# Attention scores in parts of five and one chunk, maxima over three operands, later biases, and a last row sum on TensorE

## The chip, the core and the metric

The program runs on one NeuronCore of a Trainium2 chip. The metric is the device time of one execution in microseconds (us); the median of three executions of the kernel before is 2793.07 us (2792.54 to 2796.49). All arithmetic is 32-bit floating point. Engine names follow the profile: PE is TensorE's matmul side (PEld its weight loads), DVE VectorE, ACT ScalarE, POOL GpSimd, SP the engine that issues most of the loads.

## The reference, cut to what matters

Four blocks follow each other on `x` of 16 batches, 100 tokens and 512 channels. Each adds its output, times the tanh of a gate, to `x`: cross-attention with 16 heads (called a0 below), a mixture of eight experts with two per token, cross-attention with 8 heads (a1), and a feed-forward layer with dequantized weights. Each works on the layer-normalized `x`. The context of 722 rows and 384 channels is the same for both attentions. What the change touches is the attention:

```python
q = layernorm(x) @ Wq + bq          # a1 has no bq, bk, bv
k = ctx @ Wk + bk                   # 722 keys per batch
v = ctx @ Wv + bv
attn = softmax(q @ k.T * D**-0.5)   # over the 722 keys, per head
x = x + tanh(g) * ((attn @ v) @ Wo + bo)
```

## The kernel before, in words

**Tiling.** The 1600 tokens lie in 13 tiles of 128 rows (the last has 64). The 722 keys of a batch are six chunks (`NS`), five of 128 keys and one of `SL` = 82. A *step* is one pair of batch `b` and 128-channel block `m`; 16 batches by 4 blocks are 64 steps in each attention. A block holds `G` heads: four in a0, two in a1.

**One step.** `scores(b, m, part)` multiplies keys by queries, so that keys lie on the partitions and the 100 tokens on the free side. Part 0 has chunks 0 to 2, part 1 has chunks 3 to 5 (`NS2` = 3). Each part takes one PSUM tile `ps_s` with one bank per head (a0 has one such tile, a1 two). ACT copies it to the SBUF tile `raw` (L379, and L385 and L388 for part 1; L388 is the chunk of 82), and a DVE reduction (L391) takes the greatest over the chunks. The result of part 0 is put between the chunks, so that the reduction of part 1 goes over four operands and gives `mx`. `peaks` (L393) transposes `mx` on PE (`ps_mx`, L399) and reduces to one maximum for each token and head. `softmax` (L407) transposes the maxima back to all partitions (`ps_top`, L413), subtracts them in two DVE instructions of three chunks (L417), takes the exponential on ACT (L423), and adds the six chunks on POOL to `sm` (L426, five adds). `attend` (L431) multiplies by the values (L438), sums `sm` over the partitions with a matmul by ones (L447), and divides on DVE (L455, L456). The rows of the last chunk past 82 hold a very negative number, so their exponential is zero.

**The order.** PE's order is the order in which the program is written. On the other engines the framework's scheduler orders the instructions when the program is built; an instruction handed to `keep_in_program_order` keeps its written place. Every engine executes its queue in order. `run` (L490) writes the steps one behind the other: iteration `i` has `peaks(i)`, part 0 of the scores of step `i+1`, filler units, `softmax(i)` (in a0), part 1 of the scores, `attend(i-1)`, further filler units. In a1 both score parts and `attend` stand ahead of the first fillers and `softmax`. The fillers are keys and values of the next batches (L210, L232), queries (L334), the query inputs (L314) and `project` (L458), the output projection of a tile with its addition to `x`. Units with a due step are in `extra`; the others are dealt out by a planner so that each step gets an equal share of matmul columns:

```python
whole = sum(map(self.cost, todo + sum((extra[j] for j in range(i, end)), [])))
share = whole / max(1, end - i)
```

with `end` = 62. The first units with at least 2000 columns of a step go to the first place (`u[0]`), the others to the second (`u[1]`). All of these take PSUM tiles of the pool `ps_m`, which has four buffers. `project` of the tiles that batch `b` completes stands at step `4(b+1)+1`; in a0 the layer norm and the routing logits of that tile for the experts follow it (`after_project`).

**Biases.** `add_bias` (L330) adds the gated output bias to a tile of `x` on POOL. In a0 each `query_input` calls it right behind its normalization. In a1 the first four tiles get it as units of step 3. The gated bias is made by `output_bias` (L298) on PE and DVE.

Of the kernel before, what the change touches and what calls it, by code (L numbers as in the profile page):

```python
# [16 lines left out]
P = 128  # L17
B, T, C = 16, 100, 512
# [5 lines left out]
KC = C // P  # L24
KK = CK // P
NS = -(-S // P)
SL = S - (NS - 1) * P
NS2 = NS // 2
GB = 4
GT = GB * T  # L30
EPS = 1e-5
# [19 lines left out]
def bcast(ap, *shape):  # L51
    return ap.to_broadcast(list(shape))
# [7 lines left out]
def rows_of(i):  # L60
    return P if i < NTT - 1 else NL
# [81 lines left out]
class Attention:  # L143
# [167 lines left out]
            nc.vector.tensor_tensor(self.gbo, ps, self.gbo, ALU.add)  # L311
        nc.vector.tensor_scalar(self.gbo, self.gbo, self.gate, None, ALU.mult)

    def query_input(self, i, on_act=False):  # L314
        net, nc, n = self.net, self.net.nc, rows_of(i)
        xn = self.p2.tile([P, C], F32, tag="xn", name=f"xn_{self.name}_{i}")
        if on_act:
            nc.scalar.activation(
                xn,
                net.x[:, i, :],  # L320
                AF.Identity,
                bias=net.shift[:, i : i + 1],
                scale=net.rstd[:, i : i + 1],
            )
        else:
            net.normalized(nc.gpsimd, xn, i)
            self.add_bias(i)
        net.transposed(self.ps_m, self.tT[:, :, i * P : i * P + n], xn[:n])

    def add_bias(self, i):  # L330
        x = self.net.x[:, i, :]
        self.net.nc.gpsimd.tensor_tensor(x, x, self.gbo, ALU.add)

    def queries(self, g, m, lo=0, hi=GT):  # L334

# [22 lines left out]
    def scores(self, b, m, part):  # L358


        nc, D, G = self.net.nc, self.D, self.G
        g, i = divmod(b, GB)
        q = slice(i * T, (i + 1) * T)
        ps = self.ps_s.tile([P, G, 512], F32, tag="s", name="ps_s")
        for n in range(NS2):
            c = part * NS2 + n
            r = P if c < NS - 1 else SL
            for j in range(G):
                nc.tensor.matmul(  # L369
                    ps[:r, j, n * T : (n + 1) * T],  # L370
                    self.kT[b, m][j * D : (j + 1) * D, c * P : c * P + r],
                    self.qT[g][j * D : (j + 1) * D, m, q],
                    start=True,
                    stop=True,
                )

        st = self.raw[(b * KC + m) % 2]
        if part == 0:
            nc.scalar.copy(  # L379
                st[:, :, :NS2, :].rearrange("p g c t -> p g (c t)"), ps[:, :, : NS2 * T]  # L380
            )
            greatest, of = st[:, :, NS2, :], st[:, :, :NS2, :]
        else:
            n = NS2 - 1
            nc.scalar.copy(  # L385
                st[:, :, NS2 + 1 : NS, :].rearrange("p g c t -> p g (c t)"), ps[:, :, : n * T]
            )
            nc.scalar.copy(st[:SL, :, NS, :], ps[:SL, :, n * T : NS2 * T])  # L388
            self.mx[b, m] = self.p2.tile([P, G, T], F32, tag="mx", name="mx", bufs=1)
            greatest, of = self.mx[b, m], st[:, :, NS2:, :]  # L390
        nc.vector.tensor_reduce(greatest, of.rearrange("p g c t -> p g t c"), AX.X, ALU.max)  # L391

    def peaks(self, b, m):  # L393

# [12 lines left out]
    def softmax(self, b, m):  # L407

        nc, G = self.net.nc, self.G
        top, st = self.top.pop((b, m)), self.raw[(b * KC + m) % 2]  # L410
        ps = self.ps_m.tile([P, G, T], F32, tag="mm", name="ps_top")
        for j in range(G):
            nc.tensor.transpose(ps[:, j, :], bcast(top[:, j : j + 1], T, P), self.net.ident[:T, :T])  # L413
        t = self.p2.tile([P, 2, G, NS2, T], F32, tag="pT", name="pT")
        sm = self.p2.tile([P, G, T], F32, tag="sm", name="sm")
        for part in range(2):
            nc.vector.tensor_tensor(  # L417
                t[:, part],
                st[:, :, part * (NS2 + 1) : part * (NS2 + 1) + NS2, :],
                bcast(ps.unsqueeze(2), P, G, NS2, T),  # L420
                ALU.subtract,
            )
            nc.scalar.activation(t[:, part], t[:, part], AF.Exp)  # L423
            for n in range(NS2):
                if part or n:
                    nc.gpsimd.tensor_tensor(  # L426
                        sm, t[:, part, :, n, :], sm if part or n > 1 else t[:, 0, :, 0, :], ALU.add
                    )
        self.pT[b, m] = t, sm

    def attend(self, b, m):  # L431
        nc, D, G = self.net.nc, self.D, self.G
        t, sm = self.pT.pop((b, m))
        ps = self.ps_m.tile([P, 2, T], F32, tag="mm", name="ps_pv")
        for c in range(NS):
            n = P if c < NS - 1 else SL
            for j in range(G):
                nc.tensor.matmul(  # L438
                    ps[j * D : (j + 1) * D, 0, :],
                    self.v[b][:n, c, m * P + j * D : m * P + (j + 1) * D],  # L440
                    t[:n, c // NS2, j, c % NS2, :],
                    start=(c == 0),
                    stop=(c == NS - 1),
                )

        for j in range(G):
            nc.tensor.matmul(  # L447
                ps[j * D : (j + 1) * D, 1, :],
                self.net.ones[:, :D],
                sm[:, j, :],  # L450
                start=True,
                stop=True,
            )
# [36 lines left out]
    def run(self, done=(), after_project=None, more=()):  # L490
# [8 lines left out]
        for g in range(1, B // GB):  # L499
            at = 4 * KC * (g - 1)  # L500
# [27 lines left out]
        for i in range(-1, len(steps)):  # L528
            b, m = steps[max(i, 0)]
# [841 lines left out]
def tile_flamingo(ctx: ExitStack, tc: tile.TileContext, a: dict, out: bass.AP):  # L1371
    nc = tc.nc
# [15 lines left out]
    a0 = Attention(net, "a0", a["ctxT"], w0, tgx[:, 0:1], heads, extremes)  # L1388
    a1 = Attention(net, "a1", a["ctxT"], w1, tgx[:, 1:2], 8)
# [3 lines left out]
    with ExitStack() as cm:  # L1393
        pc = cm.enter_context(tc.tile_pool(name="moe_c", bufs=1))
        with ExitStack() as c0:
# [25 lines left out]
            with tc.manual_schedule(engines={PE}):  # L1421
                a0.first_keys()
                for f, *u in gates:
                    f(*u)
                for i in range(4):
                    net.moments(i)
                net.norm_scales(0, 4)
                for c in range(4):
                    a0.values(0, c)
                    if c == 2:  # L1430
                        a0.output_bias()
                for i in range(4):
# [12 lines left out]
                more = [(-1, a0.queries, 0, m) for m in range(1, KC)]  # L1445
                more += [(0, a0.values, 0, c) for c in range(4, NS)]
                a0.run((), after_project, more)

        with ExitStack() as c1:
# [3 lines left out]
            with ExitStack() as cw:  # L1453
                moe.open_weights(cw, 0)
                moe.open_rows(cw)
                with ExitStack() as cr:
                    ps = open_pool(cr, tc, "route_p", 6, space=PSUM)
# [10 lines left out]
                    with tc.manual_schedule(engines={PE}):  # L1468
                        late = range(LATE, NTT)
# [12 lines left out]
                        to = moe.places(ps, pn)  # L1482
# [9 lines left out]
                with tc.If(nc.values_load(flag[0:1, 0:1], min_val=0, max_val=1) > 0):  # L1492
                    guarded_attention(net, a["x"], a["ctxT"], w0, tgx[:, 0:1], heads, o_s, x_s)
                    with ExitStack() as cg:
                        p2 = cg.enter_context(tc.tile_pool(name="again_2", bufs=2))
                        pn = cg.enter_context(tc.tile_pool(name="again_n", bufs=1))
                        ps = cg.enter_context(tc.tile_pool(name="again_p", bufs=4, space=PSUM))
# [9 lines left out]
                        to = moe.places(ps, pn)  # L1507
# [99 lines left out]
```

## Time and profile before

| | |
|---|---|
| median of three runs | 2793.07 us |
| profiled execution | 2793.14 us |
| its span, first to last instruction | 2791.4 us |
| mean granted TensorE clock | 0.983 |
| PE busy | 2697.3 us (97%) |
| DVE, ACT, POOL busy | 1166.8, 855.9, 692.2 us |

Stages by the timeline, from the span's start: a0 to about 933 us, routing to about 980, the experts to about 1610, a1 to about 2418, the feed-forward layer to the end.

The page of a profile gives busy times and groups of instructions. A group's line has the count, the busy time, the mean duration of one in ns, and the idle time of the engine just before, with what ended it. A timeline row has start, length, engine, line, operation, and in brackets the idle time before it. The view of waits has in each row the waiting engine and line, what it waited for, the total in us, the number of waits and the longest. A window row has the stretch, its length, and for PE, PEld, DVE, ACT and POOL the busy time with the number of instructions, then the granted clock, the DMA share and GB/s.

### The profile page before, as it was taken

Reading aid. Unit: us, or ns where it says so; the run is one execution under the profiler, and the core shown is the slowest. Engines: PE = TensorE matmul, PEld = TensorE weight load, DVE = VectorE, ACT = ScalarE, POOL = GpSimd, SP = SyncE. Lnnn points to the kernel's source line nnn. Section 1 sums busy time; section 2 is a strip of 40 time slices with the busy share of each in tenths; the row PEclk is TensorE's granted clock in tenths of the full one; section 3 lists DMA queues with packets and bytes.
Section 4 is the critical chain, followed back from the end, with each engine's and each line's share of the span. In section 5 each row is a group of like instructions: output and inputs, shape, how many; then the busy total and the mean of one; then the engine's idle time right before and its main releaser. Section 6 shows DMA issues by size and latency. Waiting matters only on the chain. (4 is left out here: it accounts for less than half of the span.)

```text
span 2791.4 us, 45251 instructions
## 1 busy us (share of the span) xinstructions
PE 2697.3 (97%) x19536; PEld 1742.5 (62%) x19536; DVE 1166.8 (42%) x1449; ACT 855.9 (31%) x1322; POOL 692.2 (25%) x821
## 2 busy tenths in 40 slices
PE   8999999999998899999999989999999999799999
PEld 4565566566555588888878855666666666445554
DVE  4676767766667400000000056544444444521100
ACT  2445454444445100000000035433333334211110
POOL 3433434343333100000000054223222222401000
PEclk9999999999999899999999999999999999899999
DMA  4000100010001399999999522100001010430000
GB/s 155 25 17 18 33 25 25 17 44 18 17 29 43 121 342 344 318 314 319 317 319 310 189 77 59 36 17 18 32 17 33 17 33 1 146 95 15 12 12 10
DMA packets 129892, 278.31 MB, mean 100 GB/s; under 512 B 5825, under 2 KB 5841, under 8 KB 129169
## 3 DMA queue, kind: packets, MB, share of 16 engines
q1 hardware_dynamic: 117888, 246.80, 25.7%
q0 software_dynamic: 5088, 16.28, 1.8%
q10 hardware_dynamic: 6704, 12.19, 1.2%
q8 instruction: 159, 2.61, 0.4%
q14 instruction: 53, 0.43, 0.1%
HBM read 260.31 MB, written 14.94 MB: 99 GB/s over the span
## 5 line engine op out<-in xcount | busy, mean ns | idle before, releaser
L241 PE MATMUL ps_v<-wv_a,ctx_a 128*128 128x512 f32 (+1 forms) x1152 | 521.5, 600 | 0.4 <-PEq L923 0.4
L216 PE MATMUL ps_k<-ctx_a,wk_a 128*128 128x361 f32 x1488 | 487.2, 475 | 0.7 <-DVE tT_a L140 0.7
L426 POOL TENSOR_TENSOR sm<-pT,sm 128x400 f32<-128x400 f32 (+1 forms) x512 | 420.1, 820 | 44.2 <-ACT pT L423 4.8
L865 PE MATMUL ps_h<-xT,w 128*128 128x128 f32 x3712 | 422.1, 276 | 3.8 <-DVEq L1492 3.8
L865 PEld LDWEIGHTS ps_h<-xT,w 128*128 128x128 f32 x3712 | 419.5, 193 | 4.5 <-ACTq L1492 4.0
L216 PEld LDWEIGHTS ps_k<-ctx_a,wk_a 128*128 128x128 f32 x1488 | 274.7, 191 | 162.2 <-issue 20.1
L241 PEld LDWEIGHTS ps_v<-wv_a,ctx_a 128*128 128x128 f32 (+1 forms) x1152 | 205.6, 185 | 243.0 <-issue 234.0
L426 POOL TENSOR_TENSOR sm<-pT 128x400 f32<-128x400 f32 (+1 forms) x128 | 105.2, 822 | 928.4 <-ACT pT L423 928.3
L391 DVE TENSOR_REDUCE mx<-raw_a 128x400 f32<-128x1600 f32 (+1 forms) x128 | 287.2, 2244 | 80.2 <-ACT raw_a L388 74.0
L423 ACT ACTIVATE pT<-pT 128x1200 f32<-128x1200 f32 (+1 forms) x256 | 239.9, 953 | 260.5 <-DVE pT L417 260.1
L417 DVE TENSOR_TENSOR pT<-raw_a,ps_top 128x1200 f32<-128x1200 f32 (+1 forms) x256 | 268.0, 1085 | 33.0 <-PE ps_top L413 32.3
L369 PE MATMUL ps_s<-qT_a,kT_a 32*128 32x100 f32 (+3 forms) x4608 | 215.3, 279 | 2.9 <-ACT raw_a L379 1.6
L391 DVE TENSOR_REDUCE raw_a<-raw_a 128x400 f32<-128x1200 f32 (+1 forms) x128 | 152.0, 1187 | 138.6 <-ACT raw_a L379 138.3
L885 PE MATMUL ps_o<-w,midT 128*128 128x512 f32 x464 | 203.9, 592 | 0.0
L369 PEld LDWEIGHTS ps_s<-qT_a,kT_a 32*128 32x128 f32 (+3 forms) x4608 | 181.3, 181 | 35.9 <-issue 23.5
L876 DVE TENSOR_TENSOR midT<-silu,ps_h 128x512 f32<-128x512 f32 x58 | 39.9, 687 | 389.8 <-PE ps_h L865 389.8
L248 ACT COPY v_a<-ps_v 128x512 f32<-128x512 f32 x192 | 111.8, 584 | 292.7 <-PE ps_v L241 290.0
L1091 PE MATMUL ps_z<-ffn_w,y_ffn 128*128 128x512 f32 (+1 forms) x416 | 190.8, 594 | 0.0
L1073 PE MATMUL ps_y<-hT,ffn_w 128*128 128x384 f32 (+2 forms) x512 | 184.1, 504 | 0.0
L438 PE MATMUL ps_pv<-pT,v_a 128*32 128x100 f32 (+3 forms) x4608 | 163.7, 255 | 6.8 <-ACT pT L423 6.8
L837 POOL DMA_INDIRECT xt<-xn_d,map_i x29 | 27.5, 950 | 567.0 <-PE ps_xT L850 525.5
L379 ACT COPY raw_a<-ps_s 128x1200 f32<-128x1200 f32 (+1 forms) x128 | 116.3, 908 | 134.7 <-PE ps_s L369 133.2
(164 smaller groups left out, 2159.0 us busy)
## 6 DMA issues: line engine op xcount, KB each, us to landing
w<-in_L_ffn_w SPq DMA_DIRECT2D x116, 1024.0 KB, 6.5
w<-in_L_ffn_wo SPq DMA_DIRECT2D x29, 2048.0 KB, 10.5
ctx_a<-in_ctxT SPq DMA_DIRECT2D x30, 1083.0 KB, 5.4
q<-in_L_ffn_fc_q SPq DMA_DIRECT2D x8, 1024.0 KB, 5.0
ffn_w<-in_L_ffn_fc_scales SPq DMA_DIRECT2D x8, 1024.0 KB, 10.2
rows<-ot ACTq DMA_DIRECT2D x29, 256.0 KB, 6.8
xn_d<-xn_moe ACTq DMA_DIRECT2D x12, 256.0 KB, 2.0
ctx_a<-in_ctxT SPq DMA_DIRECT2D x6, 361.0 KB, 8.5
```

Source lines behind the costliest of these rows:

```text
L216: nc.tensor.matmul(ps, self.wk[:, k, m * P : (m + 1) * P], self.cxs[b][:, k, c * SH : (c + 1) * SH], start=(k == 0), stop=(k == KK - 1),)
L241: nc.tensor.matmul(ps[:n], self.cxs[b][:, k, c * P : c * P + n], self.wv[:, k, :], start=(k == 0), stop=(k == KK - 1),)
L369: nc.tensor.matmul(ps[:r, j, n * T : (n + 1) * T], self.kT[b, m][j * D : (j + 1) * D, c * P : c * P + r], self.qT[g][j * D : (j + 1) * D, ...
L391: nc.vector.tensor_reduce(greatest, of.rearrange("p g c t -> p g t c"), AX.X, ALU.max)
L417: nc.vector.tensor_tensor(t[:, part], st[:, :, part * (NS2 + 1) : part * (NS2 + 1) + NS2, :], bcast(ps.unsqueeze(2), P, G, NS2, T), ALU.su ...
L423: nc.scalar.activation(t[:, part], t[:, part], AF.Exp)
L426: nc.gpsimd.tensor_tensor(sm, t[:, part, :, n, :], sm if part or n > 1 else t[:, 0, :, 0, :], ALU.add)
L438: nc.tensor.matmul(ps[j * D : (j + 1) * D, 0, :], self.v[b][:n, c, m * P + j * D : m * P + (j + 1) * D], t[:n, c // NS2, j, c % NS2, :], s ...
L865: nc.tensor.matmul(ph[:, f, :], w[:, n, k, f * P : (f + 1) * P], self.xT[j][:, k, :], start=(k == 0), stop=(k == KC - 1),)
L885: nc.tensor.matmul(po, self.midT[j, f // 4][:, f % 4, :], w[:, f, :], start=(f == 0), stop=(f == KF - 1),)
L1073: nc.tensor.matmul(ps[:, :nt], w1[f // nf][:, k, f % nf * P : (f % nf + 1) * P], hT[g][:, k, :nt], start=(k == 0), stop=(k == KC - 1),)
L1091: nc.tensor.matmul(z[j][:n], y[:, j * P : j * P + n], w2[f // nf][:, f % nf, :], start=(f == 0), stop=(f == NF - 1),)
```

## The change

- **Scores.** Part 0 has five chunks (40 PE instructions in a0 for 24, since each product is two instructions in the trace), part 1 the last one. ACT copies part 0 with one instruction of 500 columns per head, part 1 with the copy of 82 rows.
- **Maxima.** Two reductions over three operands follow part 0 (chunks 0 to 2 into a slot; that slot with chunks 3 and 4 into `mx`). Part 1 adds one `tensor_tensor` maximum of `mx` and the last chunk.
- **Subtraction.** The second half is two instructions (two chunks, one chunk), since a slot lies between them now.
- **Last sums.** In the last two steps of an attention (`late`) POOL adds nothing; PE sums all six chunks by matmuls with ones.
- **Biases.** The first four tiles get theirs at steps 3 (tiles 0, 1) and 4 (tiles 2, 3), in both attentions, in written order on POOL.
- **Projection.** The tile that batch 14 completes (tile 10) is projected at step 63, no more at 61; in a0 its moments, scales, normalization, transposes and logits move by two with it.

```diff
-    def query_input(self, i, on_act=False):
+    def query_input(self, i, on_act=False, bias=True):
...
-            self.add_bias(i)
+            if bias:
+                self.add_bias(i)
...
-    def add_bias(self, i):
+    def add_bias(self, i, pin=False):
         x = self.net.x[:, i, :]
-        self.net.nc.gpsimd.tensor_tensor(x, x, self.gbo, ALU.add)
+        ins = self.net.nc.gpsimd.tensor_tensor(x, x, self.gbo, ALU.add)
+        if pin:
+            self.net.tc.keep_in_program_order(ins)
...
-        for n in range(NS2):
-            c = part * NS2 + n
-            r = P if c < NS - 1 else SL
+        r = SL if part else P
+        for n, c in enumerate((NS - 1,) if part else range(NS - 1)):
             for j in range(G):
                 nc.tensor.matmul(
...
-        if part == 0:
-            nc.scalar.copy(
-                st[:, :, :NS2, :].rearrange("p g c t -> p g (c t)"), ps[:, :, : NS2 * T]
-            )
-            greatest, of = st[:, :, NS2, :], st[:, :, :NS2, :]
-        else:
-            n = NS2 - 1
-            nc.scalar.copy(
-                st[:, :, NS2 + 1 : NS, :].rearrange("p g c t -> p g (c t)"), ps[:, :, : n * T]
-            )
-            nc.scalar.copy(st[:SL, :, NS, :], ps[:SL, :, n * T : NS2 * T])
-            self.mx[b, m] = self.p2.tile([P, G, T], F32, tag="mx", name="mx", bufs=1)
-            greatest, of = self.mx[b, m], st[:, :, NS2:, :]
-        nc.vector.tensor_reduce(greatest, of.rearrange("p g c t -> p g t c"), AX.X, ALU.max)
+        if part:
+            nc.scalar.copy(st[:SL, :, NS, :], ps[:SL, :, :T])
+            mx = self.mx[b, m]
+            nc.vector.tensor_tensor(mx, mx, st[:, :, NS, :], ALU.max)
+            return
+        nc.scalar.copy(st[:, :, :NS1, :].rearrange("p g c t -> p g (c t)"), ps[:, :, : NS1 * T])
+        mx = self.mx[b, m] = self.p2.tile([P, G, T], F32, tag="mx", name="mx", bufs=1)
+        for c, to in ((0, st[:, :, NS1, :]), (3, mx)):
+            nc.vector.tensor_reduce(
+                to, st[:, :, c : c + 3, :].rearrange("p g c t -> p g t c"), AX.X, ALU.max
+            )
...
+        late = b == B - 1 and m >= KC - 2
+        sm = None if late else self.p2.tile([P, G, T], F32, tag="sm", name="sm")
         for part in range(2):
-            nc.vector.tensor_tensor(
-                t[:, part],
...
+            for c, z, at in ((0, 3, 0),) if part == 0 else ((0, 2, 3), (2, 3, NS)):
+                nc.vector.tensor_tensor(
+                    t[:, part, :, c:z, :],
+                    st[:, :, at : at + z - c, :],
+                    bcast(ps.unsqueeze(2), P, G, z - c, T),
+                    ALU.subtract,
+                )
             nc.scalar.activation(t[:, part], t[:, part], AF.Exp)
-            for n in range(NS2):
+            for n in () if late else range(3):
...
+        parts = [sm] if sm is not None else [t[:, c // 3, :, c % 3, :] for c in range(NS)]
+        for k, of in enumerate(parts):
+            for j in range(G):
+                nc.tensor.matmul(
+                    ps[j * D : (j + 1) * D, 1, :],
+                    self.net.ones[:, :D],
+                    of[:, j, :],
+                    start=(k == 0),
+                    stop=(k == len(parts) - 1),
+                )
...
-                at = (b + 1) * KC + 1
+                at = (b + 1) * KC + (1 if b != B - 2 else KC - 1)
...
-                    a0.query_input(i)
+                    a0.query_input(i, bias=False)
...
+                more += [(3 + i // 2, a0.add_bias, i, True) for i in range(4)]
...
-            more += [(3, a1.add_bias, i) for i in range(4)]
+            more += [(3 + i // 2, a1.add_bias, i, True) for i in range(4)]
```

More of the change, by code (lines that the diff above doesn't have):

```diff
@@ L27 @@
 SL = S - (NS - 1) * P
-NS2 = NS // 2
+NS1 = NS - 1
 GB = 4
@@ L413, in softmax @@
             nc.tensor.transpose(ps[:, j, :], bcast(top[:, j : j + 1], T, P), self.net.ident[:T, :T])
-        t = self.p2.tile([P, 2, G, NS2, T], F32, tag="pT", name="pT")
-        sm = self.p2.tile([P, G, T], F32, tag="sm", name="sm")
+        t = self.p2.tile([P, 2, G, 3, T], F32, tag="pT", name="pT")
+        late = b == B - 1 and m >= KC - 2
+        sm = None if late else self.p2.tile([P, G, T], F32, tag="sm", name="sm")
         for part in range(2):
-            nc.vector.tensor_tensor(
-                t[:, part],
-                st[:, :, part * (NS2 + 1) : part * (NS2 + 1) + NS2, :],
-                bcast(ps.unsqueeze(2), P, G, NS2, T),
-                ALU.subtract,
-            )
+            for c, z, at in ((0, 3, 0),) if part == 0 else ((0, 2, 3), (2, 3, NS)):
[5 more added lines that the diff above has]
+                )
             nc.scalar.activation(t[:, part], t[:, part], AF.Exp)
-            for n in range(NS2):
+            for n in () if late else range(3):
                 if part or n:
@@ L440, in attend @@
                     self.v[b][:n, c, m * P + j * D : m * P + (j + 1) * D],
-                    t[:n, c // NS2, j, c % NS2, :],
+                    t[:n, c // 3, j, c % 3, :],
                     start=(c == 0),
@@ L444, in attend @@
                 )
[L446 to L453, printed above, removed]
+        parts = [sm] if sm is not None else [t[:, c // 3, :, c % 3, :] for c in range(NS)]
[8 more added lines that the diff above has]
+                )
         rs = self.p2.tile([P, T], F32, tag="rs", name="rs")
```

## The prediction

> **What bounds the kernel now.** First the page's busy times and clock:
>
> ```profile
> PE 2697.3 (97%) x19536; PEld 1742.5 (62%) x19536; DVE 1166.8 (42%) x1449; ACT 855.9 (31%) x1322; POOL 692.2 (25%) x821
> PEclk9999999999999899999999999999999999899999
> ```
>
> PE is the bound, so only its idle time and its half-clock time can be won: summed over the trace 89.9 us of gaps, and a clock of 0.983. Next, PE's waits:
>
> ```profile
> PE ps_mx L399 <- DVE mx L391: 33.7, 31, 6.3
> PE ps_pv L447 <- POOL sm L426: 22.3, 10, 8.7
> PE ps_pv L438 <- ACT pT L423: 6.8, 7, 1.8
> ```
>
> The change works on all three. By windows, 25.4 us of the waits ahead of `ps_mx` lie between 60 and 887 us, in a0's steps; nearly all of the rest at the ends of a0 and a1. The timeline of the worst step (step 4) shows the chain:
>
> ```profile
> 114.96 2.72 DVE L417 TENSOR_TENSOR pT<-raw_a,ps_top 128x1200 f32<-128x1200 f32 x2
> ...
> 116.46 1.20 ACT L423 ACTIVATE pT<-pT 128x1200 f32<-128x1200 f32 x1 [1.35 <-DVE pT L417]
> ...
> 117.57 0.81 ACT L385 COPY raw_a<-ps_s 128x800 f32<-128x800 f32 x1
> ...
> 118.27 1.20 ACT L423 ACTIVATE pT<-pT 128x1200 f32<-128x1200 f32 x1
> ...
> 119.38 0.48 ACT L388 COPY raw_a<-ps_s 82x400 f32<-82x400 f32 x1
> ...
> 119.89 2.90 DVE L391 TENSOR_REDUCE mx<-raw_a 128x400 f32<-128x1600 f32 x1 [1.22 <-ACT raw_a L388]
> ...
> 122.84 1.09 PE L399 MATMUL ps_mx<-ident,mx 128*100 128x128 f32 x4 [3.82 <-DVE mx L391]
> ```
>
> Part 1's last copy stands behind both exponentials, and a 2.9 us reduction follows: 12.2 us from one `peaks` (110.64) to the next operand. Durations come from the groups by shape:
>
> ```profile
> L391 DVE TENSOR_REDUCE mx<-raw_a 128x400 f32<-128x1600 f32 x64 | 189.2, 2957 | 74.0 <-ACT raw_a L388 74.0
> L417 DVE TENSOR_TENSOR pT<-raw_a,ps_top 128x1200 f32<-128x1200 f32 x128 | 173.7, 1398 | 17.7 <-PE ps_top L413 17.5
> L391 DVE TENSOR_REDUCE raw_a<-raw_a 128x400 f32<-128x1200 f32 x64 | 98.0, 1532 | 66.7 <-ACT raw_a L379 66.5
> L417 DVE TENSOR_TENSOR pT<-raw_a,ps_top 128x600 f32<-128x600 f32 x128 | 94.2, 772 | 15.3 <-PE ps_top L413 14.8 <-POOL x L332 0.3
> L379 ACT COPY raw_a<-ps_s 128x1200 f32<-128x1200 f32 x64 | 74.1, 1158 | 97.7 <-PE ps_s L369 96.3 <-PE ps_k L216 1.4
> L385 ACT COPY raw_a<-ps_s 128x800 f32<-128x800 f32 x64 | 51.7, 807 | 3.1 <-PE ps_s L369 3.1
> ```
>
> **The clock, a rule weighed.** Windows around two of the waits:
>
> ```profile
> 797.00:801.90 4.90, 2.10 (x20) 1.14 (x22) 3.15 (x2) 2.28 (x5) 4.06 (x4) 1.00 0.01 2
> 802.00:805.30 3.30, 3.30 (x27) 2.54 (x20) 1.69 (x3) 1.16 (x1) 0.77 (x1) 0.50 0.00 0
> 856.00:860.00 4.00, 2.03 (x31) 1.23 (x29) 3.76 (x9) 0.56 (x1) 1.30 (x2) 0.99 0.00 0
> 860.00:863.40 3.40, 3.40 (x4) 1.44 (x5) 2.71 (x7) 1.16 (x1) 0.00 (x0) 0.51 0.02 5
> ```
>
> After gaps of 2.80 and 1.97 us PE ran at half rate for 3.4 us, losing 1.7 us each. The Trainium skill ("TensorE: Matmul & The Clock Gate", section "Why this matters for your kernels") warns of gaps above about 3 us. By that rule only the 3.82 us gap (half rate from 122.7 to 129.5) costs, 3.3 us; by the rows 6.7. I follow the rows: shortened gaps of 2 us still count as dangerous.
>
> **Part 1: a0's steps.** New chain. `peaks` 0.53; part 0's 40 instructions at 24 in 0.93: 1.55; to the copy 0.12; the copy, by the slope from 800 to 1200 elements (0.88 ns each), 1.86; two reductions 3.06; subtractions 1.40, and by their slope (1.04 ns, 0.15 fixed) 0.98 and 0.56: 2.94, behind the reductions since these are written first; the maximum, 0.56 by the same slope. The last copy (0.47) is ready under the subtractions. With 0.05 for the semaphore: 10.7 us.
>
> Here a rule speaks against the change. The skill ("SBUF — State Buffer", section "SBUF: two separate sides") says that a DVE operation with two SBUF inputs and a POOL operation exclude each other for a whole instruction. The subtraction has one input in PSUM; the new maximum has both in SBUF and meets POOL's adds (1.04 us each). The trace has one such meeting:
>
> ```profile
> 1640.86 4.54 POOL L332 TENSOR_TENSOR x<-x,gbo_a 128x512 f32<-128x512 f32 x3 [3.77 <-DVE gbo_a L312]
> 1641.63 1.43 DVE L948 SCALAR_TENSOR_TENSOR x<-r,probs,x 128x512 f32<-128x512 f32 x1
> 1651.99 0.60 PE L447 MATMUL ps_pv<-sm,ones 128*64 128x100 f32 x4 [8.74 <-POOL sm L426]
> ```
>
> 0.74 alone became 1.43. By the page the loss is 0 to 1.04, by the row 0.69; I take 0.6: chain 11.3 us.
>
> PE's own step is `peaks` and part 0 (2.1), `ps_top`, part 1 and `attend` (0.44 + 0.3 + 1.35 = 2.1), and fillers at 0.842 ns per column (0.431 us per 512). It waits where 4.2 + fillers < 11.3, below 8430 columns. Working the planner's rule through for both versions: moving `project` out of `range(i, end)` lightens the tail. New columns: step 4 4844 (as before), 57 7522, 58 7010, 59 8310: waits 3.0 + 0.8 + 1.2 + 0.1 = 5.1. The 25.4 us become 5: **−20.3**. The page's worst case (chain 11.7) gives back 4, no meeting wins 2.
>
> Clock: 6.7 lost now; step 4 still gaps: **−4.5** (−3.3 to −6.7).
>
> What is late next: `ps_top` is held until the subtractions end, now 8.1 us after part 0 instead of about 6. In eleven steps with three or four short fillers the third may come for its buffer at 7.6. From 0 to 11 us; I take **+5**, since rotation is not visible in the rows.
>
> Part 1's matmuls in a0 need the only `ps_s` back: copy done at 0.12 + 1.86 + 0.05 = 2.03 after part 0; with one key filler PE comes at 2.29 (72.83 to 75.12). Hidden by 0.26; 0 to +5, taken as 0. In a1 two tiles exist, `peaks` waits nowhere in mid-stage, and the extra DVE instructions (0.35 for the maximum, 0.15 for the split) lie in a queue that is busy about half of the time: nothing.
>
> **Part 2: a0's start.** POOL's normalization of tile 2 began at 38.93 behind two biases (36.46, 2.49 us); PE waited 2.99 and 0.78. Without them the copies of tiles 0 and 1 on DVE end at 38.95, two more (0.69 each) at 40.3, queries start at 40.4 instead of 42.20: 1.8. PE ran at clock 0.53 from 41 to 48; one of its two half stretches should go, 1.7. **−3.5** (−1.8 to −4.8). At steps 3 and 4 the biases take 2.6 us each of a POOL queue that has 5.2 us of adds and 2.1 of query input in a step of 8 to 13; the sum made there is wanted one step later, so they are hidden; uncovered they would cost up to 5.
>
> **Part 3: a0's end,** 885.0 to 933.5 us, 48.5 us now: 26.8 of full-rate work, 12.8 waits, 8.9 half clock. New: sums on PE, 48 instructions for 8, about 0.85 each: 28.5. Waits: step 61 has 4332 columns, 3.4; step 63's part 1 behind the long copy with no filler, 1.6 (0.53 now); `peaks` of 63 3.8 (4.72 now); exponentials 1.7; `turn` of tile 10, whose moments, scales (ACT table load 1.28) and POOL pass now stand right ahead of it, 1.2. POOL's 3.56 goes; `project` fills step 63. Two table loads (896.4 and 903.3, 1.28 each) leave ACT's way between the exponentials. The store of the normalized tile on ACT's queue (2.0 us to landing) moves too; the gathers that read it start at 966.6, some 20 us behind. Half clock about 5. **−3** (−8 to +3).
>
> **Part 4: a1's start.** The five adds (0.68 each) can begin at 1642 instead of 1645.4; with two gathers (0.96) between them they end at 1647.3, not 1652: 4.7 less. Half rate then meets 5 us of work, +0.8; biases at step 4, a short step whose POOL idle is 1.55 against 2.6 us, +1. **−3** (−8 to +2).
>
> **Part 5: a1's end,** 2379.97 to 2409.64, 29.7 us.
>
> ```profile
> 2397.19 0.67 PE L399 MATMUL ps_mx<-ident,mx 128*100 128x128 f32 x2 [6.32 <-DVE mx L391]
> ```
>
> New: work 15.9 with PE sums; step 61's sum, still on POOL and with less filler ahead, 2.1; exponentials 3.6; feed-forward work on DVE between 1; half clock 3: 25.6, **−4** (−8 to +3). PE sums are in this work with 24 instructions for 4, 0.8 a step. SP's feed-forward loads start behind the last keys, as now (2387.5), and are first used at 2420: hidden.
>
> **Sum:** −20.3 − 4.5 + 5 − 3.5 − 3 − 3 − 4 = −33.3. Against the profiled execution, 2793.1 (span 2791.4 and 1.7 around it; the median is 2793.07): **2760 us**.
>
> **Rivals.** *DVE is the new wait:* the division (0.77 + 0.26) goes ahead of the maximum, chain 12.3. By the same table of steps the waits are 16, the buffers 11: 2777. For: DVE carries about 9 of 13 us in series. Against: the maximum is written first.
>
> *All stays covered:* −25.4 − 6.7 − 4.8 − 6 − 5 − 6, no buffer holds: 2739. Against: step 4's 4844 columns.
>
> *Slower: the last copy is queued on ACT behind the second exponential* in a0. Then it ends 9.9 us after part 0, the chain is 13.2, waits 44 us over 40 steps; with re-throttling and later buffers 2805. It decides from a chain of 13.1. For: ACT's queue is rebuilt. Against: above, the copy of 800 precedes that exponential, and the new copy is ready earlier.
>
> *It doesn't do what it says:* the rebuilt queues move the waits to other steps, 2793.
>
> **How the numbers follow.** 2760 case 0.56 (its own range 2749 to 2772), DVE 0.18, all covered 0.12, slower 0.10, no change 0.04. A measurement tells 0.2%, 5.6 us, from no change. Faster 0.86, same 0.04, slower 0.10. The range 2742 to 2786 leaves out the slower and unchanged cases and part of the covered one.
>
> **What would show it.** Right: `ps_mx` waits of about 5 us between 60 and 887; the 8.74 at a1's start halved; no wait on `sm` at either end. Wrong: over 12 us there, waits of `ps_k` or `ps_v` on `pT` or `rs`, `ps_s` waiting on `raw` in many steps, a copy of 82 rows behind the second exponential.

## The result, and the profile after

The changed kernel takes 2776.5 us (median; 2775.1 to 2779.0) against 2793.0: a ratio of 0.9939, 95% interval 0.9922 to 0.9957. It is faster by 16.5 us where 33.3 were forecast; the range of 2742 to 2786 holds it. The profiled execution's span fell from 2791.4 to 2774.3 us. First the page's busy times and clock, as shown of before:

```profile
PE 2695.3 (97%) x19656; PEld 1746.7 (63%) x19656; DVE 1091.4 (39%) x1705; ACT 859.8 (31%) x1194; POOL 685.1 (25%) x801
PEclk9999999999999999999999999999999999899999
```

DVE lost 75 us of work, but PE is the bound as before, and its mean clock rose only from 0.983 to 0.985. PE's waits (us in total, times, longest us):

```profile
PE ps_pv L452 <- POOL sm L429: 14.2, 8, 5.1
PE ps_mx L399 <- DVE mx L384: 11.9, 6, 3.7
PE ps_s L372 <- ACT raw_a L386: 11.5, 4, 4.4
PE ps_pv L441 <- ACT pT L426: 9.3, 7, 3.4
...
PE ps_k L216 <- DVE pT L420: 2.1, 2, 1.9
PE ps_y L467 <- DVE pT L420: 1.9, 1, 1.9
```

The 33.7 us on the maximum are 11.9 now, and the sums fell from 22.3 to 14.2. But the third row is nearly new: part 1 of the scores waits 11.5 us for the copy of part 0 to empty the only `ps_s`. The waits on exponentials grew from 6.8 to 9.3, and the last two rows are `ps_top` buffers that come free late. In all, PE's gaps fell from 89.9 to 74.5 us.

Step 4, whose timeline was shown of before, now runs so:

```profile
104.20 0.60 PE L399 MATMUL ps_mx<-ident,mx 128*100 128x128 f32 x4
...
106.22 1.83 ACT L386 COPY raw_a<-ps_s 128x2000 f32<-128x2000 f32 x1 [1.26 <-PE ps_s L372]
...
108.08 1.54 DVE L389 TENSOR_REDUCE raw_a<-raw_a 128x400 f32<-128x1200 f32 x1 [0.66 <-ACT raw_a L386]
...
109.32 0.49 ACT L382 COPY raw_a<-ps_s 82x400 f32<-82x400 f32 x1 [0.21 <-PE ps_s L372]
109.54 1.39 DVE L420 TENSOR_TENSOR pT<-raw_a,ps_top 128x1200 f32<-128x1200 f32 x1
...
110.86 1.53 DVE L389 TENSOR_REDUCE mx<-raw_a 128x400 f32<-128x1200 f32 x1
...
112.30 1.46 DVE L420 TENSOR_TENSOR pT<-raw_a,ps_top 128x800 f32<-128x800 f32 x2
...
113.68 1.21 DVE L384 TENSOR_TENSOR mx<-mx,raw_a 128x400 f32<-128x400 f32 x1
...
114.94 0.64 PE L399 MATMUL ps_mx<-ident,mx 128*100 128x128 f32 x4 [2.38 <-DVE mx L384]
```

The last copy is done at 109.8, under the first subtraction and ahead of both exponentials. From one `peaks` to the next it is 10.74 us instead of 12.2, and the gap is 2.38 instead of 3.82 (forecast: chain 11.3, gap 3.0). One subtraction stands between the reductions; as all are in series on DVE, the sum is the same. The groups by shape give the unit costs:

```profile
L389 DVE TENSOR_REDUCE mx<-raw_a 128x400 f32<-128x1200 f32 x64 | 97.9, 1529 | 0.4
L420 DVE TENSOR_TENSOR pT<-raw_a,ps_top 128x400 f32<-128x400 f32 x128 | 71.8, 561 | 0.0
L384 DVE TENSOR_TENSOR mx<-mx,raw_a 128x400 f32<-128x400 f32 x64 | 59.4, 928 | 0.1
...
L386 ACT COPY raw_a<-ps_s 128x2000 f32<-128x2000 f32 x64 | 116.8, 1825 | 102.1 <-PE ps_s L372 90.9 <-POOL xn_moe L124 7.6 <-PE ps_top L413 3.6
```

The copy at 1.83, the short subtractions at 0.56 each and the reduction at 1.53 are as estimated. The maximum averages 0.93. The last row also shows the surprise: 7.6 us of the copy's idle time end with `xn_moe`, a tile that has nothing to do with the scores.

Where the 17.1 us of the span went, by marks in both traces (steps counted from 0: a0 from its first score to its last projection, a1's start to the `peaks` of its step 12, its middle to that of its step 60). "Half-clock loss" is PE's busy time in stretches of granted clock 0.5, divided by two:

| stage | forecast | span | PE gaps | half-clock loss |
|---|---|---|---|---|
| before a0's first score | -3.5 | -5.2 | 8.6 to 7.3 | 3.0 to 0 |
| a0's steps and end | -22.8 | -18.5 | 40.2 to 31.5 | 14.0 to 7.4 |
| the mixture-of-experts stage | 0 | +0.5 | 5.2 to 4.9 | 6.1 to 6.1 |
| a1's start | -3 | +2.9 | 19.7 to 14.8 | 3.3 to 11.0 |
| a1's middle | 0 | -0.3 | 0 to 0.6 | 0 to 0 |
| a1's end and the feed-forward layer | -4 | +3.4 | 16.3 to 15.5 | 6.5 to 7.8 |

So a0 gave most of what was expected, and a1 gave none of its 7 us and took 6 more. Over the whole span the clock gave next to nothing: its loss is 32.9 us before and 32.3 after, while the gaps shrank by 15.4. Single traces are compared here to tenths; the last section shows that the clock alone moves a stage by several us from one execution to the next.

### The profile page after: what moved, and what is told of

Read it like the earlier page. It is cut to its first block, busy times and chain, and to the rows that moved or that the text cites. A ratio compares the mean times of both kernels' runs of the same rounds, so it can differ in the third digit from the quotient of the medians.

```text
span 2774.3 us, 45812 instructions
## 1 busy us (share of the span) xinstructions
PE 2695.3 (97%) x19656; PEld 1746.7 (63%) x19656; DVE 1091.4 (39%) x1705; ACT 859.8 (31%) x1194; POOL 685.1 (25%) x801
## 5 line engine op out<-in xcount | busy, mean ns | idle before, releaser
L216 PE MATMUL ps_k<-ctx_a,wk_a 128*128 128x361 f32 x1488 | 494.0, 479 | 2.1 <-DVE pT L420 2.1
L429 POOL TENSOR_TENSOR sm<-pT,sm 128x400 f32<-128x400 f32 (+1 forms) x496 | 406.9, 820 | 68.4 <-ACT pT L426 32.7
L420 DVE TENSOR_TENSOR pT<-raw_a,ps_top 128x400 f32<-128x400 f32 (+4 forms) x384 | 279.0, 769 | 15.8 <-PE ps_top L413 14.8
L386 ACT COPY raw_a<-ps_s 128x2000 f32<-128x2000 f32 (+1 forms) x128 | 180.3, 1409 | 165.5 <-PE ps_s L372 153.8
L372 PE MATMUL ps_s<-qT_a,kT_a 32*128 32x100 f32 (+3 forms) x4608 | 214.6, 278 | 13.2 <-ACT raw_a L386 11.5
L441 PEld LDWEIGHTS ps_pv<-pT,v_a 128*32 128x32 f32 (+3 forms) x4608 | 136.0, 121 | 25.0 <-ACT pT L426 11.1
```

What stands on the lines that cost most here:

```text
L216: nc.tensor.matmul(ps, self.wk[:, k, m * P : (m + 1) * P], self.cxs[b][:, k, c * SH : (c + 1) * SH], start=(k == 0), stop=(k == KK - 1),)
L372: nc.tensor.matmul(ps[:r, j, n * T : (n + 1) * T], self.kT[b, m][j * D : (j + 1) * D, c * P : c * P + r], self.qT[g][j * D : (j + 1) * D, ...
L386: nc.scalar.copy(st[:, :, :NS1, :].rearrange("p g c t -> p g (c t)"), ps[:, :, : NS1 * T])
L420: nc.vector.tensor_tensor(t[:, part, :, c:z, :], st[:, :, at : at + z - c, :], bcast(ps.unsqueeze(2), P, G, z - c, T), ALU.subtract,)
L429: nc.gpsimd.tensor_tensor(sm, t[:, part, :, n, :], sm if part or n > 1 else t[:, 0, :, 0, :], ALU.add)
L441: nc.tensor.matmul(ps[j * D : (j + 1) * D, 0, :], self.v[b][:n, c, m * P + j * D : m * P + (j + 1) * D], t[:n, c // 3, j, c % 3, :], start ...
```

## The experiments

Each kernel was timed beside the kernel before; the median of that one was 2792.3 to 2794.1. None leaves out any of the computation.

**The scores alone.** The changed kernel with everything but the parts, the maxima and their subtractions put back:

```diff
-        late = b == B - 1 and m >= KC - 2
+        late = False
...
-                at = (b + 1) * KC + (1 if b != B - 2 else KC - 1)
+                at = (b + 1) * KC + 1
...
-                    a0.query_input(i, bias=False)
+                    a0.query_input(i)
...
-                more += [(3 + i // 2, a0.add_bias, i, True) for i in range(4)]
...
-            more += [(3 + i // 2, a1.add_bias, i, True) for i in range(4)]
+            more += [(3, a1.add_bias, i) for i in range(4)]
```

> Only the new parts of the scores (five chunks and one), the maxima over three operands and the subtractions that follow from them; biases, last sums and the projection of tile 10 as before. Theory (the parts of the scores carry the gain of a0's steps, some 13 us between the first score and the last sixteen steps, and touch nothing at the ends): 2780 us, 2776 to 2785, with waits on the new copy of part 0 of about 10 us. Rival (the gain comes from where the fillers now lie, because the projection of tile 10 was moved): 2790 or more.

Measured: 2781.2 us, ratio 0.9961 (0.9948 to 0.9975). The theory holds: 11.3 us of the change's gain are the scores' own; the 55 steps of a0 from the `peaks` of step 5 to that of step 60 took 739.3 us, as in the whole change (738.7; before 750.1), with 8.3 us of waits on the copy. It missed one point: the ends are not left alone. a1's start took 157.4 us instead of 154.4, although its biases stood as before. The loss of a1's start came with the scores.

**The store on another queue.** ScalarE's queue around the longest of the new waits, in the changed kernel's timeline:

```profile
773.83 1.52 POOL L124 TENSOR_SCALAR xn_moe<-x,rstd,shift 128x512 f32<-128x512 f32 x2
774.63 1.08 ACTq L642 DMA_DIRECT2D xn_d<-xn_moe  x2
775.80 1.82 ACT L386 COPY raw_a<-ps_s 128x2000 f32<-128x2000 f32 x1 [4.25 <-POOL xn_moe L124]
...
777.68 0.64 PE L372 MATMUL ps_s<-qT_a,kT_a 32*82 32x100 f32 x8 [4.40 <-ACT raw_a L386]
```

Part 0 ended at 770.9. The copy stood behind two DMA issues, which waited for POOL's normalization, which waited for POOL's sums until 773.85. The experiment changes one word:

```diff
-        nc.scalar.dma_start(self.xn_d[i * P : i * P + n, :], self.xn[i][:n])
+        nc.gpsimd.dma_start(self.xn_d[i * P : i * P + n, :], self.xn[i][:n])
```

> The changed kernel with the store of the normalized tile issued from GpSimd's queue instead of ScalarE's. Theory (the three long waits of part 1 for the copy of part 0, 3.4, 2.3 and 4.4 us, come from the copy standing behind that store in ScalarE's queue): the waits of part 1 on the copy fall from 11.5 to under 3 us in sum, and the time falls by 8 to 11, to 2766. Rival (the copy of 2000 elements is itself too long for the fillers ahead of part 1): the waits stay above 8 us and the time at 2775 to 2777.

Measured: 2767.5 us, ratio 0.9911 (0.9896 to 0.9926). The same place in its timeline:

```profile
766.58 1.80 ACT L386 COPY raw_a<-ps_s 128x2000 f32<-128x2000 f32 x1
...
768.44 0.42 PE L372 MATMUL ps_s<-qT_a,kT_a 32*82 32x100 f32 x8
768.96 1.52 POOL L124 TENSOR_SCALAR xn_moe<-x,rstd,shift 128x512 f32<-128x512 f32 x2
...
770.42 1.13 POOL L642 DMA_DIRECT2D xn_d<-xn_moe  x2
```

The copy starts 0.5 us after part 0's end (766.05), part 1 waits for nothing, and the waits on the copy fell from 11.5 to 1.1 us. The theory is shown: the copy is short enough for these fillers; what made it late stood ahead of it in ScalarE's queue.

**The biases of a1 as before.**

```diff
-            more += [(3 + i // 2, a1.add_bias, i, True) for i in range(4)]
+            more += [(3, a1.add_bias, i) for i in range(4)]
```

> The changed kernel with the four biases of a1 at step 3 as before. Theory (the move took away one wait of 8.7 us, but the adds now stand among the sums of several steps, whose short waits hold the clock at half for 22 us instead of 7): the long wait comes back, the half-clock stretches between the first and the twelfth step go, and the time is 2771 to 2776. Rival (the move gains its 3 us as forecast, and the loss of a1's start is the new maxima's): 2779 to 2782.

Measured: 2777.2 us, ratio 0.9949 (0.9936 to 0.9963); a1's start 157.4 us. Both were wrong. The long wait did not come back (the longest wait on a sum was 1.98), and nothing was lost or won: this part of the change is worth nothing once the scores are changed.

**The projection of tile 10 back at step 61.**

```diff
-                at = (b + 1) * KC + (1 if b != B - 2 else KC - 1)
+                at = (b + 1) * KC + 1
```

> The changed kernel with the projection of tile 10 back at step 61. Theory (its move mostly shifts fillers about): within 4 us of the changed kernel, 2774 to 2780. Rival (the lighter tail and the fillers it frees for the middle are what shortened the waits of a0's steps): 2784 or more, with waits on the maximum of 10 us or more between 60 and 887 us.

Measured: 2771.9 us, ratio 0.9920 (0.9906 to 0.9934). The intervals of this and of the changed kernel overlap; the stages are clearer. a0's last steps took 52.9 us instead of 56.3 (waits 8.1 instead of 12.5) and a1's end 3.3 us less. Moving the projection seems to cost about 4 us, which neither theory expected; the combinations below show a cost clear of noise. The fillers' new places in the middle changed nothing: 739.3 us against 738.7.

**Three steps' sums on TensorE.**

```diff
-        late = b == B - 1 and m >= KC - 2
+        late = b == B - 1 and m >= KC - 3
```

The row behind it, in the changed kernel's timeline of a1's end:

```profile
2364.23 3.98 POOL L124 TENSOR_SCALAR xn_ffn<-x,rstd,shift 128x512 f32<-128x512 f32 x4 [7.81 <-PE ps_k L216]
...
2368.18 0.60 POOL L429 TENSOR_TENSOR sm<-pT 128x200 f32<-128x200 f32 x1
...
2372.66 0.60 PE L452 MATMUL ps_pv<-sm,ones 128*64 128x100 f32 x4 [5.08 <-POOL sm L429]
```

> The changed kernel with the sums of the last three steps of each attention on TensorE instead of two. Theory (the wait of 5.1 us near a1's end is for GpSimd's sum of step 61, which stands behind four normalizations and a bias of the feed-forward layer): the wait goes, TensorE gets 0.85 us more in each attention, and the time falls by 3 to 5, to 2772. Rival (the exponentials of the same step are late too, or another wait takes its place): 2775 to 2779.

Measured: 2774.1 us, ratio 0.9930 (0.9916 to 0.9943). The wait is gone and the end took 3.0 us less. In the total the intervals of this and of the changed kernel overlap; in the profiled execution a0 lost 4.0 us more to the clock with about the same waits, which may hide the gain. In the end stage the theory holds, with part of the rival: 3.8 us of wait on the maximum followed in place of 1.6.

**The biases of a1 later.** The first four tiles get theirs five to sixteen steps later, all others seven.

```diff
-            more += [(3 + i // 2, a1.add_bias, i, True) for i in range(4)]
+            more += [(8 + 4 * i, a1.add_bias, i, True) for i in range(4)]
...
-                extra[at + 3 + n].append((self.query_input, i))
+                extra[at + 3 + n].append((self.query_input, i, False, self.G == 4))
+                if self.G == 2:
+                    extra[at + 10 + n].append((self.add_bias, i, True))
```

The rows behind it, in the changed kernel's timeline of a1's start:

```profile
1605.31 1.53 PE L372 MATMUL ps_s<-qT_a,kT_a 64*128 64x100 f32 x24 [0.35 <-DVE qT_a L358]
...
1611.39 0.42 PE L399 MATMUL ps_mx<-ident,mx 128*100 128x128 f32 x2 [1.70 <-DVE x L954]
...
1613.67 0.49 DVE L312 TENSOR_SCALAR gbo_a<-gbo_a,tgx 128x512 f32<-128x512 f32 x1 [0.93 <-DMA gbo_a<-in_L_xattn_bo]
...
1614.31 2.94 POOL L334 TENSOR_TENSOR x<-x,gbo_a 128x512 f32<-128x512 f32 x2 [2.03 <-DVE shift L119]
1614.35 3.45 DVE L954 SCALAR_TENSOR_TENSOR x<-r,probs,x 128x512 f32<-128x512 f32 x2
...
1624.95 0.39 PE L452 MATMUL ps_pv<-sm,ones 128*64 128x100 f32 x4 [0.91 <-POOL sm L429]
...
1635.00 0.39 PE L452 MATMUL ps_pv<-sm,ones 128*64 128x100 f32 x4 [1.92 <-POOL sm L429]
...
1662.41 0.39 PE L452 MATMUL ps_pv<-sm,ones 128*64 128x100 f32 x4 [1.98 <-POOL sm L429]
...
1673.69 1.27 PE L441 MATMUL ps_pv<-pT,v_a 128*64 128x100 f32 x12 [2.43 <-ACT pT L426]
...
1676.30 0.60 PE L452 MATMUL ps_pv<-sm,ones 128*64 128x100 f32 x4 [1.34 <-POOL sm L429]
```

> The changed kernel with all bias adds of a1's first seven tiles moved some ten steps later, out of the stretch in which the kernel waits at a1's start. Theory (the adds stand ahead of the sums on GpSimd and, with both inputs in SBUF, hold up VectorE's combining adds: two of 0.74 us took 3.45 us beside them): the waits on sums between the first and the twelfth step of a1 fall from 9.1 to under 5 us, half-clock stretches with them, and the time falls by 4 to 8, to 2770. Rival (the waits come from ScalarE's table loads and VectorE's longer queue): within 2 us of the changed kernel.

Measured: 2772.7 us, ratio 0.9930 (0.9917 to 0.9944), an interval that overlaps the changed kernel's; in the profiled execution a1's start took 150.1 us, 7.2 less. The waits on sums fell only to 7.6 us and all waits even rose from 14.8 to 15.5, so the theory's mechanism failed. The time came from the clock: the half-clock loss fell from 11.0 to 2.8 us. In part single waits on sums of 1.9 became 1.1 to 1.4. But 3.4 us of that loss lay behind the wait of 1.70 us for the first maximum (1611.39; the row names another instruction of DVE, but the maximum itself ends at 1611.34). This kernel has the same wait, at 1614.59, and no drop of the clock behind it. That part is not the biases' doing, as the last section shows.

**The old parts in a1 alone**, the new ones in a0:

```diff
+        if G == 2:
+            units = [(n, part * 3 + n) for n in range(3)]
+        else:
+            units = list(enumerate((NS - 1,) if part else range(NS - 1)))
...
+            nc.vector.tensor_reduce(greatest, of.rearrange("p g c t -> p g t c"), AX.X, ALU.max)
+            return
...
-            for c, z, at in ((0, 3, 0),) if part == 0 else ((0, 2, 3), (2, 3, NS)):
+            for c, z, at in ((0, 3, 4 * part),) if part == 0 or G == 2 else ((0, 2, 3), (2, 3, NS)):
```

> The changed kernel with the scores of a1 alone in two parts of three chunks and with the reductions and subtractions of before; a0 as in the changed kernel. Theory (the new parts cost a1 some 3 us at its start and 2 at its end, since VectorE's and ScalarE's queues are rebuilt and no wait in a1's middle was there to win): a1 from its first score to the twelfth step takes 154 to 155 us instead of 157.3, and the time is 2770 to 2773. Rival (a1's loss comes from the state in which the clock and the queues enter it): a1's start keeps its 157 us and the time is 2774 to 2778. Against both: with the biases pinned and the old parts the long wait of 8.7 us may come back, and the start take 160 us.

Measured: 2776.2 us, ratio 0.9940 (0.9926 to 0.9953), in the rival's range; but in a1 the third possibility was nearest. A long wait came back, though the start took 156.0 us, not 160:

```profile
1604.21 1.53 PE L376 MATMUL ps_s<-qT_a,kT_a 64*128 64x100 f32 x24 [0.35 <-DVE qT_a L358]
...
1616.00 0.48 DVE L312 TENSOR_SCALAR gbo_a<-gbo_a,tgx 128x512 f32<-128x512 f32 x1
...
1625.54 0.60 PE L471 MATMUL ps_pv<-sm,ones 128*64 128x100 f32 x4 [6.53 <-POOL sm L448]
```

The end kept its length (428.5 us with the feed-forward layer, against 429.1). So the pins alone do not remove the long wait. What became of it, in us from a1's first score:

| | before | old parts in a1 | changed |
|---|---|---|---|
| the bias is scaled (L312) | 11.8 | 11.8 | 8.4 |
| the first sum is done on POOL | 23.5 | 21.3 | 19.6 |
| PE comes for it | 14.8 | 14.8 | 18.7 |
| PE waits | 8.7 | 6.5 | 0.9 |

The pins bring the first sum forward by 2.2 us and the new parts by 1.7 more; in DVE's queue, rebuilt because of them, the scaling stands earlier (at 7.9 with the scores alone), but no run moved it by itself. The other half of the lost wait is no gain: PE, with the same instructions to do, comes 3.9 us later, 3.4 of it by half clock behind the wait of 1.70 us.

**Combinations.** The store on POOL's queue with the projection at step 61; these two with the late biases; and these three with three steps' sums on TensorE:

> The changed kernel with both the store of the normalized tile on GpSimd's queue and the projection of tile 10 back at step 61. Theory (the two gains, 9 and 4 us, are in different stages, and the wait of 5.8 us for the copy of part 0 near 885 us goes too): 2757 to 2763. Rival (with the projection at step 61 the end of a0 has its own wait on the maximum, which comes back when the copy is early): 2765 to 2768.

> The changed kernel with three of the earlier edits together: the store of the normalized tile on GpSimd's queue, the projection of tile 10 at step 61, and the bias adds of a1's first seven tiles some ten steps later. Theory (they act on different stages and add up; the late biases keep a1's start near 150 us): 2747 to 2752. Rival (a1's start depends on how the clock and the queues enter it, and the 7 us of the late biases do not come again): 2754 to 2758.

> The same three edits, and the sums of the last three steps on TensorE. Theory (with the projection back at step 61 no wait at a1's end is for a sum any more, so the third step only adds 0.85 us in each attention): 1 to 3 us above the kernel with three edits. Rival (the sums also take GpSimd work away from the feed-forward layer's normalizations, which then come earlier): 2 to 4 us below it.

Measured: 2756.1 us (ratio 0.9866, 0.9851 to 0.9881), 2752.9 us (0.9845, 0.9831 to 0.9858) and 2752.2 us (0.9847, 0.9834 to 0.9861). Store and projection together win 20.4 us against the changed kernel, more than the 9 and 5 of each alone. With the store moved, the projection's place is worth 11 us (2767.5 to 2756.1), clear of noise. The theory is right in part: with the projection at step 61 a further wait for the copy, 5.8 us at 885, stood behind that store, and 1.9 of it is left. But the wait on the maximum behind it grew from 1.5 to 4.4 us, as the rival had it, so most of the surplus is in no wait and stays unexplained. The late biases then brought only 3 us, and the intervals overlap: a1's start took 154.3 and 155.2 us, with 14.4 and 13.6 us of waits but 8.5 and 10.2 of half-clock loss. That lies between theory and rival. The third step of sums made no difference: 2.5 us less of waits at a0's end, but at a1's end PE then waited 3.1 us for a normalization of the feed-forward layer. The three edits together beat both kernels, by 41 us the one before.

**The store alone, on the kernel before** (the one-word edit above):

> The kernel before with nothing but the store of the normalized tile moved to GpSimd's queue. Theory (the store stood in ScalarE's way only with the long copy and the single buffer behind it; before, part 1 waited 1.3 us for the copy in all these steps): 2789 to 2793. Rival (the store held up ScalarE's work in the kernel before as well, and its gain has nothing to do with the change): 2782 to 2786.

Measured: 2788.1 us, ratio 0.9981 (0.9972 to 0.9990), just outside the theory's range. From the `peaks` of step 5 to that of step 60 it won 7.0 us, 3.1 of waits and 3.9 of clock. The store was in the way before too, but cost 5 us there and 9 with the long copy behind it. With the store out of the way in both kernels, the change is worth about 20 us (ratios 0.9981 and 0.9911) instead of 16.5.

## Why the forecast was right in sign and twice too large

By the stages, the gain falls 16 us short of the forecast: 4.3 in a0, 5.9 in a1's start and 7.4 in a1's end with the feed-forward layer, less 1.7 that a0's start gave beyond it. The rival "DVE is the new wait" was put at 2777, which is the time measured; since its mechanism did not happen, that is chance.

**Part 1, waits on the maximum (-20.3): right.** Between 60 and 887 us, 6.4 us are left on the maximum and 1.2 behind an exponential; 2.8 of it is the wait at 878.8 that the forecast counted at a0's end. That leaves 4.8 where 5.1 were worked out. The sum is better than its terms: the waits behind steps 4, 57, 58 and 59 are 2.4, 0, 1.2 and 1.3 for 3.0, 0.8, 1.2 and 0.1. "DVE is the new wait" (the division ahead of the maximum) did not happen: at step 4 the maximum ends at 114.9 and the division starts at 114.81.

**Part 1, the maximum beside POOL's adds (+0.6): right, a little high.** The 128x400 maximum took 1.21 us at step 4, where POOL was adding, and 0.57 where it was not; its mean is 0.93, so 0.36 is lost on average. The Trainium skill's rule of exclusive access ("SBUF — State Buffer", section "SBUF: two separate sides") agrees with these rows, and a1's start has its dearest case: two adds on DVE of 0.74 each took 3.45 us beside two on POOL that took 2.94.

**Part 1, buffers (+5): right.** Keys, values and the projection waited 4.5 us for `ps_top`'s buffer, at 439 and 607 us above all.

**Part 1, the wait for `ps_s` ("0 to +5, taken as 0"): the step that failed.** It cost 11.5 us, 10 more than before. The working took the copy from its operand (2.03 us after part 0) and compared it with PE's filler (2.29); it did not ask what stands ahead of the copy in ScalarE's queue. The store was looked at only for the gathers that read its data, and only at a0's end. With the store elsewhere the original assumption holds: 1.1 us. Of the shortfall in the total this explains less than the 10 us of waits suggest, some 4 us, since 5 of the 9 that the store cost were there before the change.

**Part 1, the clock (-4.5): too large.** In these steps it gained 1.0 us, since waits on the copy and on buffers dropped the clock where the maximum used to. By the rule of the Trainium skill that the prediction weighed ("TensorE: Matmul & The Clock Gate", section "Why this matters for your kernels": gaps above about 3 us) waits of 1.9 us at 439 and 607 would be harmless; each dropped it in some executions, so following the rows was right.

**Part 2 (-3.5): -5.2**, just beyond the bound of 4.8: no half-clock stretch was left in that execution, where one was counted. The scores alone, with the biases in place, start at 47.9 us; the ten with them moved at 42.5 to 44.2, those near 44.2 with one such stretch.

**Part 3, a0's end (-3), and what is left of a0.** In the forecast's own terms a0 was -20.3 - 4.5 + 5 - 3 = -22.8 and measured -18.5. Its waits fell by 8.7 us and its clock loss by 6.6; TensorE's sums added 1.6. The remaining -5 us stand in no recorded wait, but in the transposes of `peaks`, on which PE spent 33.8 us in a0 before and 29.1 after. Each first transpose that PE reaches without waiting starts 0.16 us before the recorded end of the matmul ahead of it: 31 of the 64 before, 58 after. So a wait cost 0.16 us more than its row says. The scores alone left a0's last stretch at 60.2 us, as before (60.6); with the late sums it takes 52.9, and with the projection moved as well 56.3. Late sums are thus worth about 7 us there, and "`project` fills step 63" took half of it back.

**Part 4, a1's start (-3): wrong, +2.9.** The step that failed is the credit of 4.7 us to the moved biases: they are worth nothing beside the new parts. The long wait did go, half of it because PE came later; but from 8.7 us in one piece the kernel went to a row of waits of 0.9 to 2.4, and the clock loss rose from 3.3 to 11.0 us. Most of the long wait's half-clock stretch was idle anyway: PE was busy in 3.3 us of its 10.2.

**Part 5, a1's end (-4): wrong, +1.9, and the feed-forward layer +1.5, 1.2 of it clock.** Step 61's sum, set at 2.1, cost 5.1: on POOL four normalizations of the feed-forward layer stood ahead of it and a bias add of that layer among its own. The moved projection cost 3.3 us of this stage; with it back at step 61 the end took 51.8 us against 52.9 before, so the forecast was too large even then.

## What to carry to other kernels

When a single buffer comes to depend on a longer copy, list everything ahead of that copy in its engine's queue, DMA issues that wait for data of other stages included; moving one such store won 9 us here, 5 of which it had cost the kernel before as well. Several waits of 2 us can cost more than one of 8, since each can drop the clock anew: count waits, not only their sum. And edits that rebuild automatically ordered queues should be timed one at a time: by their stages, three of the five parts here gave the gain (scores with maxima, a0's biases, late sums), one gave nothing (a1's biases) and one took 4 us or more back (the projection).

## What was not expected of the hardware

The same wait does not always drop the clock. Windows right behind the wait of 3.4 us for the copy, first in the changed kernel, then in the one with late biases in a1, whose a0 has the same instructions in the same order:

```profile
391.39:394.80 3.41, 3.41 (x70) 2.58 (x71) 3.41 (x3) 3.26 (x4) 0.00 (x0) 1.00 0.02 5
439.35:446.20 6.85, 6.85 (x20) 3.67 (x21) 3.92 (x8) 1.65 (x2) 5.75 (x6) 1.00 0.00 0
```

```profile
391.80:395.20 3.40, 3.40 (x45) 2.40 (x36) 3.40 (x5) 2.63 (x3) 0.66 (x1) 0.50 0.02 5
439.60:446.40 6.80, 5.90 (x7) 2.53 (x8) 3.19 (x7) 1.87 (x2) 6.49 (x6) 0.50 0.00 0
```

After gaps of 3.37 and 3.39 us the clock (the third figure from the end) was full in one and half in the other; so it was around the gap of 1.94 us at 440. In five executions with this same a0 the 55 steps in its middle had about 18 us of waits each and lost 5.7, 7.2, 9.7, 9.6 and 3.3 us to the clock.

The traces show where the difference comes from. All 365 changes of the clock in the thirteen traces lie on a grid of 3.413 us, to 0.001 us; only where the grid lies against the program differs from one execution to the next. Windows cut on that grid, again in the two kernels:

```profile
386.37:389.78 3.41, 1.65 (x9) 0.94 (x7) 1.57 (x2) 0.27 (x1) 2.61 (x4) 1.00 0.17 64
389.78:393.19 3.41, 1.80 (x65) 1.54 (x66) 1.82 (x2) 3.27 (x4) 0.00 (x0) 1.00 0.26 94
```

```profile
384.96:388.37 3.41, 2.56 (x18) 1.53 (x14) 1.08 (x3) 0.66 (x2) 3.33 (x4) 1.00 0.00 0
388.37:391.79 3.42, 0.87 (x32) 0.77 (x36) 1.56 (x2) 2.62 (x3) 0.21 (x1) 1.00 0.41 153
```

In the changed kernel a grid line cut the gap into 1.76 and 1.61 us, and the clock stayed full; in the other 2.54 us of it fell into one period, and the next ran at half. The wait of 1.70 us at a1's start fell into one period in the changed kernel and was cut into 0.87 and 0.83 in the one with late biases. Over all traces, each of the 102 full-clock periods with 2.0 us or more of idle PE was followed by half clock, none of the 130 with 0.5 to 1.0 us, and 61 of the 163 between. So it matters how a wait falls, and 3.4 of the 7 us of the late biases were such luck.

Idle time is not the whole rule. The pair at 440 goes against it: 1.78 us in one period kept the clock, 1.01 and 0.93 in two dropped it. And in the routing stage of every trace the clock drops once behind a period in which the records show PE never idle, busy with matmuls of 32 columns. What counts as work there stays open.
